# The blank rows of the last experts' slots written later, and the router's matrix of layer 2 on another queue

## The chip, the cores and the metric

The kernel runs on one core of a Trainium2 chip. A core has five engines that run beside each other, each with its own stream of instructions: TensorE (PE) for matrix products, VectorE (DVE), ScalarE (ACT), GpSimd (POOL) and SyncE (SP), which in this kernel only issues transfers. Transfers (DMAs) are issued by SP, ACT or POOL, each on its own queue, and are moved by 16 DMA engines. Engines wait for each other, and for transfers, on semaphores.

The metric is the device time of one execution in microseconds (us). Smaller is better.

## What is computed

A graph network of four layers on 3125 nodes of 256 features and 100000 edges. Each layer adds to the node rows `x` the outputs of a graph part, of a mixing part (linear attention), and then of a mixture of experts. The part that matters here is the expert part of layer 2, the graph and mixing parts of layer 3 that follow it, and the expert part of layer 3 at the end:

```python
def _L2_ffn_ref(x, Wr, br, W1, b1, W2, b2, gamma, beta):   # 8 experts, one batch
    logits = jnp.mean(x, axis=1) @ Wr + br
    routing_weights = jax.nn.softmax(logits, axis=-1)
    ...
    top_w, top_i = jax.lax.top_k(rw_tok, K)                # K = 2
    h = jax.nn.gelu(jnp.einsum('nd,edf->enf', xf, W1) + b1[:, None, :], approximate=False)
    y = jnp.einsum('enf,efd->end', h, W2) + b2[:, None, :]
    out = jnp.einsum('ne,end->nd', w_dense, y).reshape(B, S, D)
    return _layer_norm(out + x, gamma, beta)

def _L3_ffn_ref(h, gate_w, gate_b, w1, b1, w2, b2):        # 8 experts, capacity C
    ...
    buf = jnp.zeros((E, C, D), dtype=h.dtype).at[idx, pos_safe].set(x, mode='drop')
    hmid = jax.nn.relu(jnp.einsum('ecd,edf->ecf', buf, w1) + b1[:, None, :])
    ybuf = jnp.einsum('ecf,efd->ecd', hmid, w2) + b2[:, None, :]
    y_tok = ybuf[idx, pos_g] * (prb * kept)[:, None]
```

In layer 2 one routing decision holds for all nodes, since it is made from the mean over the nodes: two experts of eight are chosen, and all rows pass through both. In layer 3 every node goes to one expert, which has room for C = 489 nodes.

## The kernel before

The node rows stay on chip: `self.x` and `self.xn` (rows, 25 blocks of 125 nodes) and `self.xt` (the normalised rows turned, features on the partitions). Work on nodes goes in pieces of 500 nodes (`PIECES`), the last of 125. The source states operations in one order; a scheduler of the language then places the instructions of each engine, and it may move an instruction ahead of others of its engine where its inputs allow. What it has placed, the engine runs in that order.

`run` calls `l1_ffn`, whose last part is the graph and mixing work of layer 2, and then `l3_ffn`. `l3_ffn` does four things in this order:

1. It sets up the slots of layer 3's experts. `bx_d` in DRAM has 8 x 489 = 3912 rows of 514 numbers: the normalised row, the row itself, the weight and the node's number. Slots that no node takes must hold blank rows (zeros, and a node number out of range). One blank row is made in the tile `row` on chip (L2187, L2188, on POOL) and written to all slots of `bx_d` by two transfers on ACT's queue (L2190, L2192).
2. It defines `follow`, which routes a piece of nodes once its rows are final and scatters them into `bx_d` (L2255). It uses the same tile name `row`, of which the pool holds one buffer. So the first instruction that writes `row` again, the copy of the node numbers at L2253 (DVE), waits until the fill has read the blank row.
3. It calls `l3_gnn_mix`, which issues the loads of layer 3's weights on SP (through `l3_mix_by_pieces`, with the small columns `g1` and `b1` at L2015), then calls `l2_ffn`, and then does the graph and mixing parts of layer 3.
4. It runs the eight last experts (L2265 to L2307). For each, w1 and the slots `xb` are loaded on SP, w2 and b2 on ACT.

`l2_ffn` loads the router's matrix (L1782, on SP) and four small inputs on ACT, sums `self.mean` over the pieces (L1789), multiplies by the router's matrix (L1794), takes softmax twice and the best two (up to L975 in the helper `top2`), adds beta to `x` (`add_rows`, L982), and loads for each of the two experts W1, W2 and b1 from the place that the chosen number gives (L1819 to L1825, on SP). `expert` then runs, piece by piece, W1 (L261, PE), gelu (L1010, ACT), W2 (L1016, PE) and adds the weighted result to `y` (L1018, DVE), 25 blocks for each expert. `finish_norm` ends the layer.

Some helpers record their operations under their own lines: loads of weights L172 (`load_w`) and L179 (`load_b`), matrix products L255 and L261, copies out of PSUM L163 (DVE) and L165 (ACT), softmax L268 to L273. The sum over rows of a piece is at L1774. The loads of `cs` by layer 3's graph part are at L156.

Of the kernel before, what the change touches and what calls it, by code (L numbers as in the profile page):

```python
# [109 lines left out]
class Net:  # L110
# [1665 lines left out]
    def l2_ffn(self):  # L1776
        nc, tc, a = self.nc, self.tc, self.a
        NE = 8
        with ExitStack() as s:
            sb = s.enter_context(self.pool("f2_sb"))  # L1780
            wk = s.enter_context(self.pool("f2_wk", 2))
            wr = self.load_w(sb, "L2_ffn_Wr")  # L1782
            br = self.load_b(sb, "L2_ffn_br")
            b2 = sb.tile([NE, D], F32, name="b2")
            nc.scalar.dma_start(b2, a["L2_ffn_b2"])
            gamma = self.load_b(sb, "L2_ffn_gamma")
            beta = self.load_b(sb, "L2_ffn_beta")
            mean = sb.tile([128, HB], F32, name="mean")
            nc.vector.tensor_reduce(mean, self.mean, axis=AX.X, op=OP.add)  # L1789
            nc.vector.tensor_scalar(mean, mean, 1.0 / N, None, op0=OP.mult)  # L1790

            ps = self.bank()
            for h in range(HB):
                nc.tensor.matmul(ps[:, :NE], mean[:, h:h + 1].to_broadcast([128, 128]), wr[:, h, :],  # L1794
                                 start=(h == 0), stop=(h == HB - 1))
            rw = sb.tile([128, 1, NE], F32, name="rw")
            nc.vector.tensor_add(rw[:, 0, :], ps[:, :NE], br)
            self.softmax(sb, rw, 1, NE)
            sc = sb.tile([128, 1, NE], F32, name="sc")
            nc.vector.tensor_scalar(sc, rw, float(N), None, op0=OP.mult)  # L1800
            nc.vector.reciprocal(sc, sc)
            cap = float(-(-N * 5 // (4 * NE)))
            nc.vector.tensor_scalar(sc, sc, cap, 1.0, op0=OP.mult, op1=OP.min)
            nc.vector.tensor_mul(rw, rw, sc)
            self.softmax(sb, rw, 1, NE)
            g, tw, i8 = self.top2(sb, rw, NE, 128, 1)
            ps = self.bank()
            nc.tensor.transpose(ps[:NE, :128], g[:, 0, :], self.ident)
            gt = sb.tile([NE, 128], F32, name="gt2")
            nc.vector.tensor_copy(gt, ps[:NE, :128])  # L1810
            ps = self.bank()
            nc.tensor.matmul(ps[:P, :D], gt[:, :P], b2, start=True, stop=True)
            bb = sb.tile([P, D], F32, name="bb")
            nc.vector.tensor_copy(bb, ps[:P, :D])
            y = sb.tile([P, NB, D], F32, name="y")
            nc.vector.tensor_add(y, self.xn, self.blocks(bb))
            self.add_rows(beta)
            for j in range(2):
                e = nc.sync.value_load(i8[0:1, 0, j:j + 1], min_val=0, max_val=NE - 1)  # L1819
                w1 = wk.tile([128, HB, 512], F32, name="w1")  # L1820
                nc.sync.dma_start(w1, a["L2_ffn_W1"][ds(e, 1)].rearrange("o (c p) f -> p (o c) f", p=128))
                w2 = wk.tile([128, 4, D], F32, name="w2")
                nc.sync.dma_start(w2, a["L2_ffn_W2"][ds(e, 1)].rearrange("o (c p) f -> p (o c) f", p=128))
                b1 = wk.tile([128, 4], F32, name="b1")
                nc.sync.dma_start(b1, a["L2_ffn_b1"][ds(e, 1)].rearrange("o p f -> (o p) f"))  # L1825
                self.expert(wk, w1, b1, AF.Gelu, w2, lambda b: tw[:P, 0, j:j + 1], y)
            self.expect(1, self.norm_turn_add, 1)
            self.finish_norm(y, gamma)
# [336 lines left out]
                        nc.vector.scalar_tensor_tensor(self.x[:, b, :], t.rearrange("p h d -> p (h d)"), 0.0,  # L2165
                                                       self.x[:, b, :], op0=OP.max, op1=OP.add)

    def l3_ffn(self, before, parts):

# [5 lines left out]
        with ExitStack() as s:  # L2177
# [9 lines left out]
            nc.gpsimd.memset(blank[:, 0], 0.0)  # L2187
            nc.gpsimd.memset(blank[:, 0, WX - 1:], float(1 << 20))  # L2188
            whole = NE * CAP // 112 * 112
            nc.scalar.dma_start(bx[:whole].rearrange("(t p) d -> p t d", p=112),  # L2190
                                blank[:112, 0, None, :].to_broadcast([112, whole // 112, WX]))
            nc.scalar.dma_start(bx[whole:], blank[:NE * CAP - whole, 0])  # L2192
            place = sb.tile([P, NB], F32, name="place")
            nc.gpsimd.iota(place, pattern=[[P, NB]], base=0, channel_multiplier=1,
                           allow_small_or_imprecise_dtypes=True)
# [68 lines left out]
            tiles = [(r, min(128, CAP - r)) for r in range(0, CAP, 128)]  # L2264
            for e in range(NE):  # L2265
                w1 = self.load_w(wk, "w1", a["L3_ffn_w1"][e])
                w2 = self.load_w(wk, "w2", a["L3_ffn_w2"][e], eng=nc.scalar)
                b2 = self.load_b(wk, "b2", a["L3_ffn_b2"][e])
                xb = wk.tile([128, len(tiles), WX], F32, name="xb")
                for t, (r, n) in enumerate(tiles):  # L2270
                    nc.sync.dma_start(xb[:n, t, :], bx[e * CAP + r:e * CAP + r + n])  # L2271
                xt = wk.tile([128, HB, CAP], F32, name="xbt")
                for h in range(HB):
                    ps = self.bank()
                    for t, (r, n) in enumerate(tiles):
                        nc.tensor.transpose(ps[:, r:r + n], xb[:n, t, h * 128:(h + 1) * 128], self.ident[:n, :n])
                    self.evac(xt[:, h, :], ps[:, :CAP])
                hid = wk.tile([128, NF, CAP], F32, name="hid")
                for f in range(NF):
                    ps = self.bank()  # L2280
                    self.mm_feat(ps[:, :CAP], w1[:, :, f * 128:(f + 1) * 128], xt, 0, CAP)
                    nc.scalar.activation(hid[:, f, :], ps[:, :CAP], AF.Relu, bias=b1[:, e, f:f + 1])
                for t, (r, n) in enumerate(tiles):
                    ps = self.bank()
                    for f in range(NF):
                        nc.tensor.matmul(ps[:n, :D], hid[:, f, r:r + n], w2[:, f, :],  # L2286
                                         start=(f == 0), stop=(f == NF - 1))
                    to = wk.tile([128, 1], I32, name="to", bufs=4)
                    nc.vector.tensor_copy(to[:n], xb[:n, t, 2 * D + 1:])
                    y = wk.tile([128, D], F32, name="y")  # L2290
                    nc.vector.tensor_add(y[:n], ps[:n, :D], b2[:n])  # L2291
                    nc.vector.tensor_scalar(y[:n], y[:n], xb[:n, t, 2 * D:2 * D + 1], None, op0=OP.mult)  # L2292

                    fin = wk.tile([128, D], F32, name="fin")
                    nc.vector.tensor_scalar(fin[:n], y[:n], 0.0, 0.0, op0=OP.mult, op1=OP.is_equal)
                    num = wk.tile([128, D], F32, name="num")
                    nc.vector.tensor_tensor(num[:n], y[:n], y[:n], op=OP.is_equal)
                    sub = wk.tile([128, D], F32, name="sub", bufs=4)
                    nc.vector.tensor_scalar(sub[:n], y[:n], -1e4, 1e4, op0=OP.max, op1=OP.min)
                    nc.vector.tensor_mul(sub[:n], sub[:n], num[:n])  # L2300
                    nc.vector.copy_predicated(sub[:n], fin[:n].bitcast(U32), y[:n])  # L2301
                    nc.vector.tensor_add(sub[:n], sub[:n], xb[:n, t, D:2 * D])  # L2302
                    st = nc.gpsimd.indirect_dma_start(  # L2303
                        out=a["out"], out_offset=bass.IndirectOffsetOnAxis(ap=to[:n], axis=0),
                        in_=sub[:n], in_offset=None, bounds_check=N - 1, oob_is_err=False)
                    tc.declare_no_dep(st.ins, group="results", reason="each slot has a place of its own")
                    tc.add_to_no_dep_group("results", st.ins)  # L2307
# [32 lines left out]
    def run(self):  # L2340
        nc = self.nc
        self.prep()
        self.l0_prepare()
        self.l0_first()
        with self.pool("f0_g") as sb:
            self.l0_gates(sb)
            self.l0_gnn()
            self.l0_ffn(True)
        self.l1_ffn(self.l1_gnn_mix, self.l2_gnn_mix)
        self.l3_ffn(lambda arrivals: self.l3_gnn_mix(self.l2_ffn, arrivals), 2)  # L2350

        ps = self.bank()
        nc.tensor.matmul(ps[:, :8], self.ones, self.viol, start=True, stop=True)
        tot = self.c.tile([128, 1], F32, name="tot_v")
        nc.vector.tensor_reduce(tot, ps[:, :8], axis=AX.X, op=OP.add)
        bad = self.c.tile([128, 1], I32, name="bad_v")
        nc.vector.tensor_scalar(bad, tot, 0.0, None, op0=OP.is_gt)
        with self.tc.If(nc.values_load(bad[0:1, 0:1], min_val=0, max_val=1) != 0):
            self.general()
# [65 lines left out]
```

## Time and profile before

| what | us |
|---|---|
| median of 3 runs | 4667.59 (4659.35 to 4668.4) |
| the profiled execution | 4666.18 |
| its span, first to last instruction | 4664.4 |
| PE busy in it | 3722.3 (80%) |
| DVE busy | 2505.6 (54%) |
| ACT busy | 1302.8 (28%) |
| POOL busy | 1020.2 (22%) |

The profile comes from one execution. Its busy shares are means over stages of different kinds, so a part is read in its own stretch of time. The stages that are of interest here, in the same execution:

| stretch, us from the start | what runs |
|---|---|
| to 3251 | graph and mixing parts of layer 2 (the gathered matmuls at L1617 end here) |
| 3244 to 3279 | the blank rows are written to `bx_d` |
| 3279 to 3299 | router of layer 2 |
| 3299.5 to about 3480 | the two experts of layer 2 and the normalisation |
| 3480 to 4411 | graph and mixing parts of layer 3, routing of its pieces |
| 4411 to the end | the eight last experts |

Three kinds of lines are quoted from it. A line of windows gives, for a stretch, how long each engine was busy, the granted clock of PE as a share of full speed (PEclk), the busy share of the DMA engines, and GB/s. A line of waits names who waited, for whom, and the total, the number of times and the longest in us. A line in order of time gives start and duration in us, the engine, the line in the source, the operation with the names it writes and reads, and in brackets how long the engine stood idle before it and what ended that. A "q" behind an engine's name (ACTq, SPq) is its queue of instructions that issue transfers.

### The profile page before, as it was taken

How to read it: one execution, taken by the hardware profiler on the slowest of the kernel's cores; microseconds unless marked ns; L12 is line 12 of the kernel's file. 1: busy time of each engine (PE TensorE's matmuls, PEld its weight loads, DVE VectorE, ACT ScalarE, POOL GpSimd, SP SyncE). 2: the span in 40 equal slices, each digit the busy share in tenths (PEclk: the TensorE clock that was granted, in tenths of full speed). 3: DMA queues.
4: the chain of work that ended last, by engine and by line, in shares of the span. 5: the costliest groups of instructions: out<-in, count | busy, mean ns of one | idle time of the engine just before them, and what ended most of it. 6: DMA issues, size and time to landing. Idle time of an engine off the chain costs nothing. (4 is left out here: it accounts for less than half of the span.)

```text
span 4664.4 us, 50401 instructions
## 1 busy us (share of the span) xinstructions
PE 3722.3 (80%) x16695; PEld 2505.9 (54%) x16695; DVE 2505.6 (54%) x8604; ACT 1302.8 (28%) x2336; POOL 1020.2 (22%) x1041
## 2 busy tenths in 40 slices
PE   1887796499938799999656566766799999999698
PEld 0676695277724556555545455655464444444466
DVE  5877317544475526994322323444265666777544
ACT  1367100022213223323100000000155655555521
POOL 2000000400055000000577777775000000000011
PEclk9786896599959799999877777887899999999699
DMA  6244630244332000000333333334102222221232
GB/s 176 75 113 118 138 82 22 81 135 140 107 85 40 4 29 9 13 14 7 106 105 106 104 104 104 104 104 139 58 7 59 59 63 56 63 52 49 74 107 68
DMA packets 256035, 358.86 MB, mean 77 GB/s; under 512 B 62719, under 2 KB 199350, under 8 KB 255765
## 3 DMA queue, kind: packets, MB, share of 16 engines
q1 hardware_dynamic: 135900, 176.07, 13.1%
q0 software_dynamic: 62832, 126.93, 10.3%
q10 hardware_dynamic: 57033, 52.54, 4.2%
q8 instruction: 136, 2.23, 0.2%
q14 instruction: 134, 1.10, 0.1%
HBM read 268.73 MB, written 94.97 MB: 78 GB/s over the span
## 5 line engine op out<-in xcount | busy, mean ns | idle before, releaser
L1601 POOL DMA_INDIRECT hg<-hx_d,idx x782 | 743.3, 950 | 282.8 <-issue 214.2
L1617 PE MATMUL acc<-hg,to 128*125 128x256 f32 x2042 | 584.5, 449 | 197.9 <-DVE to L1612 192.8
L1617 PEld LDWEIGHTS acc<-hg,to 128*125 128x125 f32 x2042 | 455.4, 227 | 309.3 <-DVE to L1612 216.3
L1971 PE MATMUL acc<-z,xr 125*65 125x500 f32 (+1 forms) x1400 | 577.4, 556 | 14.3 <-DVE z L1968 13.0
L1965 ACT ACTIVATE t<-xn,us 125x1000 f32<-125x1000 f32 (+1 forms) x400 | 409.4, 1037 | 239.0 <-DVE z L1968 228.1
L1968 DVE SCALAR_TENSOR_TENSOR z<-t,us,cs 125x1000 f32<-125x1000 f32 (+1 forms) x400 | 409.3, 1028 | 115.5 <-PE acc L1971 92.6
L1971 PEld LDWEIGHTS acc<-z,xr 125*65 125x65 f32 x1400 | 188.9, 145 | 314.8 <-issue 265.5
L1605 DVE TENSOR_TENSOR kw<-hg,awt 128x8 f32<-128x8 f32 x98 | 16.4, 168 | 581.2 <-DMA hg<-hx_d,idx 513.2
L261 PE MATMUL ps<-xt,w 128*128 128x500 f32 (+1 forms) x672 | 269.0, 547 | 1.8 <-DMA w<-in_L_ffn_W_dram 1.8
L1612 DVE TENSOR_SCALAR to<-iota_w,rel_b,kw 128x125 f32<-128x125 f32 (+1 forms) x782 | 245.2, 383 | 35.6 <-PE acc L1617 28.7
L1536 DVE SCALAR_TENSOR_TENSOR junk<-iota_w,rel_b,lock 128x125 f32<-128x125 f32 (+1 forms) x782 | 248.1, 386 | 0.0
L2255 POOL DMA_INDIRECT bx_d<-row,slot x25 | 31.2, 1248 | 891.3 <-ACT t L1965 422.9
L589 PE MATMUL ps<-y,cb 125*125 125x256 bf16 x1875 | 214.7, 279 | 0.0
L589 PEld LDWEIGHTS <-cb 125*125 125x125 bf16 x1875 | 213.5, 141 | 0.1
L797 ACT ACTIVATE k<-k 125x128 f32<-125x128 f32 x50 | 15.9, 318 | 687.0 <-DVE k L796 686.9
L190 ACT ACTIVATE rstd_t<-rstd_t 125x4 f32<-125x4 f32 (+2 forms) x86 | 17.2, 203 | 645.8 <-DVE rstd_t L189 630.2
L255 PE MATMUL ps<-wo,h 128*125 128x256 f32 x800 | 187.7, 386 | 3.6 <-ACT h L1439 2.6
L243 PE MATMUL ps<-ident,xn 125*128 125x125 f32 x300 | 58.8, 347 | 159.8 <-DVE xn L209 159.7
L1445 DVE SCALAR_TENSOR_TENSOR x<-ps,lg,x 125x256 f32<-125x256 f32 x200 | 92.7, 480 | 173.6 <-PE ps L255 173.6
L261 PEld LDWEIGHTS ps<-xt,w 128*128 128x128 f32 x672 | 122.7, 193 | 114.7 <-issue 102.4
L261 PE MATMUL ps<-h,w 128*128 128x500 f32 (+1 forms) x448 | 179.5, 541 | 2.3 <-ACT h L1434 1.6
L255 PEld LDWEIGHTS ps<-wo,h 128*125 128x125 f32 x800 | 142.9, 187 | 65.9 <-ACT h L1439 43.7
(566 smaller groups left out, 6326.7 us busy)
## 6 DMA issues: line engine op xcount, KB each, us to landing
cs<-ctt_d SPq DMA_DIRECT2D x150, 218.8 KB
w<-in_L_ffn_w_dram SPq DMA_DIRECT2D x52, 512.0 KB
cnt_d<-cd SPq DMA_DIRECT2D x25, 683.6 KB
cb<-cnt_d SPq DMA_DIRECT2D x25, 683.6 KB
ctt_d<-ct ACTq DMA_DIRECT2D x6, 2734.4 KB
hg<-hx_d,idx POOLq DMA_INDIRECT x782, 2.8
b0x_d<-zero SPq DMA_DIRECT2D x1, 9984.0 KB
xb<-b0x_d SPq DMA_DIRECT2D x26, 384.0 KB
```

The costliest lines, as they stand in the source:

```text
L243: self.nc.tensor.transpose(ps[:, j * P:(j + 1) * P], src[:, i // P + j, h * 128:(h + 1) * 128], self.ident[:P, :P])
L255: self.nc.tensor.matmul(ps, xt[:, h, b * P:(b + 1) * P], w[:, h, :], start=(h == 0), stop=(h == k - 1))
L261: self.nc.tensor.matmul(ps, w[:, h, :], xt[:, h, i:i + n], start=(h == 0), stop=(h == k - 1))
L589: nc.tensor.matmul(ps[:P, :D], cf[k][:, h * P:(h + 1) * P], y3[:, b0 + k, j, :], start=(k == 0 and j == 0), stop=(k == m - 1 and j == 2))
L1445: nc.vector.scalar_tensor_tensor(self.x[:, b, :], ps[:P, :D], g[:, b, e:e + 1], self.x[:, b, :], op0=OP.mult, op1=OP.add)
L1536: nc.vector.scalar_tensor_tensor(junk[:, :m * P], self.iota_w[:, :m * P], rel[:, c:c + 1], lock[:, b:b + m].rearrange("p b n -> p (b n)"), ...
L1601: nc.gpsimd.indirect_dma_start(out=hg[:, j, :], out_offset=None, in_=hx, in_offset=bass.IndirectOffsetOnAxis(ap=idx[:, c0 + j:c0 + j + 1], ...
L1612: nc.vector.tensor_scalar(to, self.iota_w[:, :nb * P], rel[:, c:c + 1], kw[:, j:j + 1], op0=OP.is_equal, op1=OP.mult)
L1617: nc.tensor.matmul(acc[k], to[:, (k - b) * P:(k - b + 1) * P], hg[:, j, :D], start=(c == first[k]), stop=(c == last[k]))
L1965: nc.scalar.activation(t[:, :n], rows[:, k4, :n], AF.Relu, bias=us[:, 2, b, k4:k4 + 1], scale=us[:, 0, b, k4:k4 + 1])
L1968: nc.vector.scalar_tensor_tensor(z[:, :n], t[:, :n], us[:, 1, b, k4:k4 + 1], c, op0=OP.add, op1=OP.mult)
L1971: nc.tensor.matmul(acc[h, k][:, :w], xr[:, b, k4, :], z[:, k * PW:k * PW + w], start=(b == 0), stop=(b == NB - 1))
```

## The change

Four edits:

- The two transfers that write the blank rows are wrapped in a function `blank_slots`, and go on SP's queue instead of ACT's. With `later=True`, as `run` now calls it, `l3_ffn` does not issue them itself but leaves the function in `self.blank_slots`.
- `l2_ffn` calls that function after it has stated the loads for its second expert. A dependency of order alone (NoSync) on the last of these loads keeps the two transfers behind it in SP's stream; it adds no semaphore.
- The router's matrix of layer 2, `L2_ffn_Wr`, is loaded on ACT's queue instead of SP's.
- In the last experts, w2 of the second expert (`e == 1`) is loaded on SP's queue instead of ACT's.

```diff
@@ l2_ffn @@
-            wr = self.load_w(sb, "L2_ffn_Wr")
+            wr = self.load_w(sb, "L2_ffn_Wr", eng=nc.scalar)
...
-                nc.sync.dma_start(b1, a["L2_ffn_b1"][ds(e, 1)].rearrange("o p f -> (o p) f"))
+                last = nc.sync.dma_start(b1, a["L2_ffn_b1"][ds(e, 1)].rearrange("o p f -> (o p) f"))
+                if j == 1 and self.blank_slots:
+
+                    for ins in self.blank_slots():
+                        tc.add_manual_dep(ins, last.ins.name, mybir.DependencyInfo(
+                            mybir.DependencyClass.NoSync, mybir.DependencyReason.DATA), reason="weights first")
@@ l3_ffn @@
-    def l3_ffn(self, before, parts):
+    blank_slots = None
+
+    def l3_ffn(self, before, parts, later=False):
...
-            nc.scalar.dma_start(bx[:whole].rearrange("(t p) d -> p t d", p=112),
-                                blank[:112, 0, None, :].to_broadcast([112, whole // 112, WX]))
-            nc.scalar.dma_start(bx[whole:], blank[:NE * CAP - whole, 0])
+
+            def blank_slots():
+                self.blank_slots = None
+                return [nc.sync.dma_start(bx[:whole].rearrange("(t p) d -> p t d", p=112),
+                                          blank[:112, 0, None, :].to_broadcast([112, whole // 112, WX])).ins,
+                        nc.sync.dma_start(bx[whole:], blank[:NE * CAP - whole, 0]).ins]
+
+            if later:
+                self.blank_slots = blank_slots
+            else:
+                blank_slots()
...
-                w2 = self.load_w(wk, "w2", a["L3_ffn_w2"][e], eng=nc.scalar)
+                w2 = self.load_w(wk, "w2", a["L3_ffn_w2"][e], eng=nc.sync if e == 1 else nc.scalar)
@@ run @@
-        self.l3_ffn(lambda arrivals: self.l3_gnn_mix(self.l2_ffn, arrivals), 2)
+        self.l3_ffn(lambda arrivals: self.l3_gnn_mix(self.l2_ffn, arrivals), 2, True)
```

## The prediction

> **What bounds the kernel now.** I read the page first. TensorE (PE) is busy 80% of a span of 4664.4 us, so a stretch in which PE stands still is worth its length. The slices show such a stretch near 3260 us, where layer 2's expert stage begins. I then read that stretch by windows, by waits (engines, then SP's own) and in order of time.
>
> ```profile
> core 0: us, PE busy (x) PEld busy (x) DVE busy (x) ACT busy (x) POOL busy (x), PEclk, DMA share, GB/s
> 3244.00:3256.00 12.00, 7.05 (x28) 5.50 (x28) 7.94 (x21) 0.78 (x2) 0.55 (x4) 0.79 0.89 283
> 3256.00:3266.00 10.00, 0.00 (x0) 0.00 (x0) 0.00 (x0) 0.00 (x0) 0.00 (x0) 0.50 1.05 357
> 3266.00:3279.00 13.00, 0.00 (x0) 0.00 (x0) 0.00 (x0) 0.27 (x1) 0.00 (x0) 0.50 0.83 290
> 3279.00:3284.00 5.00, 0.84 (x4) 0.87 (x4) 0.85 (x4) 1.28 (x1) 0.00 (x0) 0.50 0.45 100
> 3284.00:3295.00 11.00, 0.15 (x1) 0.06 (x1) 10.13 (x31) 0.62 (x3) 0.00 (x0) 0.50 0.00 0
> ```
> For 23 us every engine is idle while the DMA engines run full; then comes a router chain with almost no DMA. The waits say on what:
> ```profile
> PE ps L1794 <- DMA L_ffn_Wr<-in_L_ffn_Wr_dram: 28.4, 1, 28.4
> ACT xt L165 <- DMA b<-in_L_ffn_b_dram: 25.1, 1, 25.1
> DVE row L2253 <- DMA bx_d<-row: 24.2, 1, 24.2
> ```
> ```profile
> SPq L2015 <- DMA bx_d<-row: 14.2, 1, 14.2
> ```
> Three engines and SP all stand behind one transfer, the blank fill of `bx_d` (7645.8 + 208.8 KB = 8.04 MB). In order of time:
> ```profile
> 3244.51 0.35 ACTq L2190 DMA_DIRECT2D bx_d<-row  x1
> ...
> 3254.80 0.29 DVE L163 COPY xt<-ps 128x125 f32<-128x125 f32 x1 [0.71 <-PE ps L243]
> ...
> 3279.24 0.17 DVE L2253 COPY row<-place 125x4 f32<-125x4 f32 x1 [24.15 <-DMA bx_d<-row]
> 3279.34 0.41 DVE L1774 TENSOR_REDUCE mean_p<-xt 128x2 f32<-128x250 f32 x1
> ...
> 3279.98 0.42 SPq L172 DMA_DIRECT2D L_ffn_Wr<-in_L_ffn_Wr_dram  x1
> ...
> 3284.67 2.35 DVE L982 TENSOR_TENSOR x<-x,L_ffn_beta 125x1024 f32<-125x1024 f32 x2
> ...
> 3295.32 0.40 SPq L1821 DMA_DIRECT2D w<-in_L_ffn_W_dram  x1
> ...
> 3299.52 9.90 PE L261 MATMUL ps<-xt,w 128*128 128x500 f32 x16 [1.84 <-DMA w<-in_L_ffn_W_dram]
> ```
> The reader should see that the input of the router (`xt`) is whole at 3255.1, its sum over rows is taken at 3279.3, and the expert's first matmul comes at 3299.5.
>
> [...] `mean` (L1774) needs nothing of `row`, yet stands 24.15 us behind it. [...] SP stood 14.2 us at L2015, and the router's matrix behind it. [...] Here the fill (ACT's queue) and layer 3's weights (SP's) moved together at 283 to 357 GB/s. [...] the trace has 0.50 in every window after 3256.
>
> **The change part by part.**
>
> *Fill off ACT's queue at 3244.5.* The wait of L2253 for it goes from in front of `mean`: in the compiled order of the changed kernel this copy stands behind the 8th accumulation `y<-ps,w,y` (L1018) of the first expert. SP's L2015 waits now for layer 3's own weights, not for the fill. These are 2.62 MB from 3248.4 on; at the 345 GB/s seen here they take 7.6 us, so SP is through by about 3260, and its next work (the expert's number) is due near 3269. Hidden, with 9 us to spare.
>
> *What is late next: the router chain.*
> - `xt` whole at 3255.1. ACT's copy of its other half no longer stands behind waits for the fill, so it comes then too.
> - L1774 to the end of L1790 took 0.82 us: 3256.0.
> - Router's matrix: now on ACT behind its copy of 3246.2 to 3246.7. It may wait for the last users of its memory, the gather stage's matmuls, which end at 3250.9. It took 3.15 us to land (3279.98 to 3283.13); in a busy stretch the 256 KB of layer 3's GNN matrix took 4.9. So it lands between 3250 and 3256: in time, within a microsecond.
> - Two matmuls to `rw` (L1797): 1.06 us, 3257.2; then L268 and L269 to the first L982: 0.48, 3257.7.
> - L982 needs beta, issued on ACT behind that copy and gamma: 3255.5. It took at most 3.47 us (3281.20 to 3284.67), so it lands at 3259.0, and the chain, which has L271 behind L982 on DVE, is held 1.3 us. I take 3259.0; with beta landing as slowly as 4.9 us it is 3260.4, with none of it 3257.7.
> - From the first L982 to the expert's weights: 3284.67 to 3295.32 = 10.65 us. The changed order still does all seven L982 ahead of L1804, so I keep it: 3269.7.
> - Weights to the first L261: 4.20 us: 3273.9. PE has been idle for 19 us, so its first 16 matmuls stay at 9.90 us rather than the 6.87 of the next piece; I count no gain there (bound: 3.0).
>
> Sum: 3299.5 - 3273.9 = 25.6 us.
>
> *Sum over rows of the last full piece (L1774, 1.19 us)* now runs ahead of L1765, in a DVE gap of 1.12 us, instead of inside the last normalisation, where it holds L191 from 3252.8 to 3253.5: 0.6 us gained, bounds 0 and 1.2.
>
> *Fill behind the second expert's weights on SP.* The three loads of the second expert begin 2.3 us after the first's and end 3.8 after them, so the fill is issued at 3273.5. The 2.10 MB of weights are ahead of it on the same queue[...]. Weights and fill together, 10.14 MB from about 3271.5 at 309 to 345 GB/s (10.7 MB moved from 3244 to 3279 is 309) end at 3301 to 3304[...]. The 8th L1018 was 30.5 us after the first L261 (3329.99), so it falls at 3304.4; the 9th, 38.9 after (3338.42), at 3312.8. DVE idles 7.95 us between them. The copy L2253 waits there for 0 to 2 us, with nothing due behind it: zero, bound 2 at the slow end[...]. Behind the fill on SP stands only `cs`, which waited 169.3 us for L1016 until 3473.84: covered. If the cover in DVE were gone, each microsecond would be one of PE[...].
>
> *w2 of layer 3's second expert from ACT to SP.* The last experts begin at 4411.05; PE's first L261 there, 4422.74, waits for `xb`, loaded by SP behind w1. On ACT, the second w2 stood behind the first w2, and SP's next w1 waited 8.6 us for a `w` until 4422.25. I take that for the first w2, still in flight; then the second had moved nothing yet and moving it gives SP no bandwidth back. If it was the second, it shared the last 1 MB of `xb`, and up to 2 us come back. On SP it now stands ahead of the second `xb`: 3.1 MB from 4422.3 at 364 to 391 GB/s land by 4431, needed at 4452. I take 0, bounds -1 (gain 2).
>
> Together 26.2 us off the profiled execution's own 4666.18 us (1.8 more than its span): 4640.0. Those runs have a median of 4667.59 (4659.35 to 4668.4), 1.4 above the profiled one; I put the forecast between the two bases, 4640.0 and 4641.4, at 4640.5.
>
> **The rivals.**
> - *Another transfer takes the fill's place (0.17).* SP's 4-byte columns at L2015, `br`, beta or the wait for freed memory in front of Wr last 6 to 16 us longer than I have them; each is on the chain one for one. For it: one load issue there took 2.78 us, and eight semaphores are shared by all loads, so one late load holds others. Against it: those delays fall beside the fill. 10 to 20 us left: 4648 to 4658, middle 4653.
> - *More than counted (0.10).* Beta in time, PE warm sooner, the `xb` head 2 us earlier: 1.3 + 3.0 + 2, saving 32: 4634.
> - *The fill holds the experts: slower (0.05).* L2253 sits between two L1018. If fill and weights need more than 41 us (from 3271.5 to 3312.8), every further microsecond stalls DVE, the banks and PE. All the gain is gone from 3339 on, that is with the 10.14 MB at 150 GB/s. At 125 GB/s it lands at 3353 and costs 40: 4666.2 - 26.2 + 40 = 4680. Against it: the three windows in which the fill ran show 283 to 357.
> - *It doesn't do what it says (0.03).* The copy in DVE or the wait in SP keeps the old order, and time stays at 4667. The compiled order speaks against it.
> - *As summed (0.65).* 20 to 30 us off: 4636 to 4647.
>
> **How the numbers follow.** About 0.2%, 9.3 us, can be told from no change. Faster: 0.65 + 0.10 + 0.16 of the first rival = 0.91. Within: 0.03 + its last 0.01 = 0.04. Slower: 0.05. The range takes in the main case, the greater gain down to 4631 and the middle of the first rival: 4631 to 4654; likeliest alone 4636 to 4647.
>
> **What would show it.** Right: DVE's wait for `bx_d<-row` is gone before 3260, L1794 starts near 3256, the first L261 of that stage near 3274, and the stage after it is as long as before. The fill runs from about 3277 to 3304 beside L1016, with L2253 behind the 8th L1018 and no DVE wait of more than 8 us before the 9th. Wrong: a wait over 5 us for a load in front of L1794, L982 or SP's L1821; a gap in PE between L1018's 8th and 9th; a later start of the last experts than 26 us ahead of before.

## The result, and the profile after

| | before | after |
|---|---|---|
| median of 5 runs, us | 4667.27 (4659.35 to 4668.4) | 4645.13 (4636.11 to 4653.43) |
| the profiled execution, us | 4666.18 | 4653.43 |
| its span, us | 4664.4 | 4651.7 |

The ratio of after to before is 0.9956, with a 95% interval of 0.994 to 0.9972: 0.28% to 0.6% less, or 13 to 28 us of 4667. Five more runs of the changed kernel, taken later beside the experiments, had a median of 4644.19 against 4668.66 for the kernel before, ratio 0.9949 (0.9937 to 0.9962).

The two profiled spans differ by only 12.7 us, less than the medians do. The changed kernel's profiled execution was already 10.4 us late when it reached the part that was changed, in code that both kernels share. So times from the start can't be laid side by side. I count instead from one event ahead of the change: the start of ACT's last square root over a whole piece (L190, 125x4), at 3243.50 before and 3253.92 after. "The stretch" below is the time from this event to the first L261 of layer 2's experts. The numbers of this table are differences of start times in the two traces (in the last row, to the end of the span), in us:

| part | before | after |
|---|---|---|
| event to `mean` (L1790) | 36.49 | 12.13 |
| event to the router's matmuls (L1794) | 39.66 | 16.32 |
| event to the first expert's weights issued (L1821) | 51.82 | 28.40 |
| event to the first L261: the stretch | 56.02 | 32.46 |
| first L261 to layer 3's first `cs` load | 174.32 | 174.17 |
| `cs` to the last scatter into `bx_d` | 934.15 | 934.29 |
| last scatter to the last experts' first L261 | 14.75 | 15.62 |
| from there to the end of the span | 241.7 | 241.2 |

The stretch became 23.56 us shorter; the four parts behind it together became 0.4 us longer. The gain is where it was looked for, and 2.6 us short of the 26.2 that were forecast.

The windows of the changed kernel (columns as before: the stretch, its length, busy us of PE, PE's weight loads, DVE, ACT and POOL, the clock, the share of the DMA engines and GB/s):

```profile
3254.00:3266.00 12.00, 6.89 (x28) 5.49 (x28) 8.79 (x25) 1.18 (x5) 0.78 (x4) 0.80 0.47 144
3266.00:3271.00 5.00, 0.76 (x4) 0.79 (x4) 0.19 (x2) 1.27 (x1) 0.00 (x0) 0.50 0.79 238
3271.00:3282.00 11.00, 0.23 (x2) 0.14 (x1) 10.08 (x32) 0.62 (x3) 0.00 (x0) 0.50 0.10 25
...
3290.00:3300.00 10.00, 10.00 (x32) 6.11 (x31) 2.74 (x3) 3.60 (x5) 0.00 (x0) 0.90 1.06 377
3300.00:3310.00 10.00, 10.00 (x33) 5.90 (x32) 1.08 (x3) 2.24 (x4) 0.00 (x0) 1.00 1.04 352
```

The 23 us in which every engine was idle are gone. What is left of them is the second line: 5 us with almost nothing on any engine while DMA runs at 238 GB/s. The fill is in the last two lines: 377 and 352 GB/s, and PE busy in all of both. The order in time shows who waited in that second line.

```profile
3258.85 0.39 SPq L172 DMA_DIRECT2D L_mix_Wq<-in_L_mix_Wq_dram  x1
...
3260.82 2.06 SPq L172 DMA_DIRECT2D L_mix_W<-in_L_mix_W_dram  x2
...
3262.40 0.40 DVE L1201 TENSOR_REDUCE wx<-wx_t 128x4 f32<-128x256 f32 x1
...
3262.88 0.39 ACTq L172 DMA_DIRECT2D L_ffn_Wr<-in_L_ffn_Wr_dram  x1
3265.51 0.44 ACTq L179 DMA_DIRECT2D L_ffn_beta<-in_L_ffn_beta_dram  x1
3266.05 0.17 DVE L1790 TENSOR_SCALAR mean<-mean 128x2 f32<-128x2 f32 x1
...
3270.24 0.99 PE L1794 MATMUL ps<-L_ffn_Wr,mean 128*128 128x8 f32 x4 [5.54 <-DMA L_ffn_br<-in_L_ffn_br_dram]
...
3271.75 1.22 DVE L982 TENSOR_TENSOR x<-x,L_ffn_beta 125x1024 f32<-125x1024 f32 x1
...
3282.32 0.40 SPq L1821 DMA_DIRECT2D w<-in_L_ffn_W_dram  x1
...
3317.10 0.16 DVE L2268 COPY row<-place 125x4 f32<-125x4 f32 x1
3325.13 0.48 DVE L1018 SCALAR_TENSOR_TENSOR y<-ps,w,y 125x256 f32<-125x256 f32 x1 [7.87 <-PE ps L1016]
```

The `mean` is there at 3266.22, the matmul with the router's matrix starts at 3270.24: 4.0 us late for the matrix. The wait names `br`, which was issued right behind it on ACT and which this matmul does not read; in the second profiled execution of this kernel (experiment 5) the same wait names the matrix. By the trace's semaphore events the matrix had landed at 3270.05. ACT issued it 0.08 us after the end of DVE's last L1201. L1201 belongs to the preparation of layer 3: it sums over `wx_t`, a tile of the pool `m3_w`, which the source closes just before `l2_ffn` opens its own pools. PE had the matrix 7.4 us after its issue, beside layer 3's weights that SP had started 4.0 to 2.1 us earlier. The last two lines are the copy that used to wait for the fill, and the accumulation after it. The copy runs without a wait, and DVE then still idles 7.87 us before its next accumulation.

### The profile page after: what moved, and what is told of

It is laid out like the page before. It is cut to its first block, busy times and chain, and to the rows that moved or that the text cites. A ratio compares the mean times of both kernels' runs of the same rounds, so it can differ in the third digit from the quotient of the medians.

```text
span 4651.7 us, 50402 instructions
## 1 busy us (share of the span) xinstructions
PE 3730.8 (80%) x16695; PEld 2512.0 (54%) x16695; DVE 2507.1 (54%) x8604; ACT 1302.0 (28%) x2336; POOL 1020.1 (22%) x1041
## 3 DMA queue, kind: packets, MB, share of 16 engines
q0 software_dynamic: 62832, 126.93, 10.4%
## 5 line engine op out<-in xcount | busy, mean ns | idle before, releaser
L1976 PE MATMUL acc<-z,xr 125*65 125x500 f32 (+1 forms) x1400 | 577.4, 555 | 14.4 <-DVE z L1973 13.1
L261 PE MATMUL ps<-xt,w 128*128 128x500 f32 (+1 forms) x672 | 268.9, 547 | 1.8 <-DMA w<-in_L_ffn_W_dram 1.8
L190 ACT ACTIVATE rstd_t<-rstd_t 125x4 f32<-125x4 f32 (+2 forms) x86 | 17.2, 203 | 648.7 <-DVE rstd_t L189 631.7
L261 PEld LDWEIGHTS ps<-xt,w 128*128 128x128 f32 x672 | 122.7, 193 | 114.6 <-issue 102.2
L261 PE MATMUL ps<-h,w 128*128 128x500 f32 (+1 forms) x448 | 179.5, 541 | 2.3 <-ACT h L1434 1.6
```

What stands on the lines that cost most here:

```text
L261: self.nc.tensor.matmul(ps, w[:, h, :], xt[:, h, i:i + n], start=(h == 0), stop=(h == k - 1))
L1976: nc.tensor.matmul(acc[h, k][:, :w], xr[:, b, k4, :], z[:, k * PW:k * PW + w], start=(b == 0), stop=(b == NB - 1))
```

## The experiments

All stretches are counted from the same event, each in its own profile. A single time says little (the five runs of the changed kernel cover 17 us), so the stretches carry the readings.

**1. Only DVE freed.** The kernel before, with the blank row in a tile of its own, so that L2253 waits for nothing:

```diff
-            blank = wk.tile([P, 4, WX], F32, name="row")
+            blank = wk.tile([P, 1, WX], F32, name="blank")
```

> Kernel before with one edit: the blank row has a tile of its own, so that the copy of node numbers into row no longer waits for the fill. The stretch read is that from ACT's last rstd of a full piece (125x4) to the first expert matmul of layer 2: 56.0 us before, 32.5 after the change. Theory A (the fill holds three queues at once: DVE's copy, ACT's copy of xt behind its small loads, SP's router matrix behind L2015): nothing is won by freeing DVE alone, stretch 54 to 57. Theory B (DVE's copy in front of the mean is what held the router): stretch 32 to 38.

The stretch was 56.6 us, as in theory A, and the time 4668.65 us against 4663.53 of the kernel before on the same chip: nothing gained. Waits in the stretch:

```profile
PE ps L1794 <- DMA L_ffn_Wr<-in_L_ffn_Wr_dram: 27.7, 1, 27.7
ACT xt L165 <- DMA L_ffn_br<-in_L_ffn_br_dram: 24.4, 1, 24.4
DVE mean_p L1774 <- ACT xt L165: 22.5, 1, 22.5
```

DVE no longer waits for `bx_d`, but for ACT's half of `xt`, for 22.5 us instead of 24.2. That copy stands on ACT behind the issue of the fill's second, small part, which got out only 22.5 us after the first (3252.80 and 3275.29 in that trace), and behind the three loads that follow it there (what these wait for is read in experiment 2). The fill held the stage by two ways at once, through the tile on DVE and through ACT's queue (and SP's L2015 besides); taking one away wins nothing.

**2. The fill left early, the router's inputs ahead of it.** Own tile as in 1, and the router's matrix, `br`, `b2` and `beta` loaded on ACT before the fill, in memory that is free then:

```diff
+    def l2_small(self, sb):
...
+            wr, br, b2, beta = self.small or self.l2_small(sb)
...
+            gamma = self.load_b(sb, "L2_ffn_gamma", eng=nc.sync)
...
+                self.small = self.l2_small(sb)
...
+            blank = wk.tile([P, 1, WX], F32, name="blank")
```

> Kernel before, the fill still early on ACT, but the blank row in a tile of its own and the router's matrix, br, b2 and beta of layer 2 loaded at the start of l3_ffn, long before; gamma on SP. So the router waits for none of its inputs, and the DMA engines are as full as before. Theory A (waits in the queues): the router comes earlier, up to what still stands behind the fill, SP's L2015 until about 35 us after the stretch's start and ACT's copy of xt behind the second part of the fill; stretch 40 to 45. Theory C (the full DMA engines themselves set the time): stretch 52 or more. If DVE and the small loads were all of it: 31 to 34.

The stretch was 43.5 us, as in theory A, and the time 4655.41 (before 4663.53). A good half of the gain comes without moving the fill, but not from the freed waits alone: with beta there early, the scheduler placed the additions (L982) ahead of the router, so that from `mean` to L975 it took 6.4 us instead of 15.4 (3.0 of which had been the wait for the matrix). ACT in order of time shows what still holds `mean`:

```profile
3251.20 0.34 ACTq L2197 DMA_DIRECT2D bx_d<-blank  x1
...
3274.32 0.48 ACTq L2199 DMA_DIRECT2D bx_d<-blank  x1
3274.84 0.27 ACT L165 COPY xt<-ps 128x125 f32<-128x125 f32 x1 [14.03 <-DMA L_mix_Wm<-in_L_mix_Wm_dram]
```

Line numbers are shifted by 7. The small second part gets out 23 us behind the first, and the last piece's `xt` copy follows it at once. What ACT waited for is named in the bracket, and it is not the fill: it is `L_mix_Wm`, a load of layer 3's weights on SP. The semaphore events of the trace say the same. The second part waited for a semaphore that this load uses too, the load landed at 3274.30, and the issue came at 3274.32. In the kernel before the two times are 3266.23 and 3266.25, in experiment 1 3275.27 and 3275.29, and there `br` and `b2` behind it waited in the same way for the two loads of `L_mix_W`. Beside the fill `L_mix_Wm` took 12.4 to 13.1 us from issue to landing in these three kernels, and 4.0 to 5.7 in the eight profiles with the fill late. So the fill slows the loads that move beside it, and these hold ACT's stream through semaphores that they share with its own transfers. This is read from the traces; no run takes the shared semaphore out alone.

SP holds the end of the stretch:

```profile
SPq L2020 <- DMA bx_d<-blank: 13.5, 1, 13.5
```
```profile
3282.21 0.17 DVE L975 TENSOR_TENSOR g<-g,h 128x8 f32<-128x8 f32 x1
...
3288.88 0.40 SPq L1825 DMA_DIRECT2D w<-in_L_ffn_W_dram  x1
```

The router has chosen at 3282.38, but the first expert's weights are issued 6.5 us later, since SP's remaining small loads had waited for the fill until 3285.26. (In the changed kernel L1821 is issued as L975 starts.) So two queues hold what is left, and not the router's inputs, which were there.

**3. Only the fill moved.** The changed kernel with the router's matrix still on SP and w2 still on ACT (the diff of `blank_slots` alone). The "second last expert" of the expectations is the second of the eight last experts, `e == 1`.

> Changed kernel with the two other edits undone: the router's matrix on SP again, w2 of the second last expert on ACT again. Theory A: the fill's move is nearly all of it; the router's matrix then stands behind layer 3's loads on SP and lands about 20 us after the stretch's start against 16.3, so stretch 34 to 38 (32.5 with the matrix on ACT, 56.0 before). Rival: the matrix's queue is what counts, stretch 50 or more. From the last scatter into bx_d to the first matmul of the last experts: 14.8 us, as before, if the moved w2 costs (15.6 after the change); no change from 15.6 if it doesn't.

The stretch was 33.6 us, just under theory A's 34 to 38, and the time 4645.48 us. So the fill's place is nearly the whole gain (22.4 us of the stretch). With the matrix on ACT the stretch is 0.4 to 1.1 us shorter (33.2 and 32.5 in two profiles of the changed kernel), hardly more than the 0.7 by which those two differ. The matrix itself came 3.7 us later here: L1794 starts 20.0 us after the event, against 16.3. Most of that does not show, because the scheduler put four of the seven additions of beta ahead of the router's first step on DVE (3266.79 to 3271.42), so fewer of them stand behind it. From the last scatter to the last experts' first L261 it took 16.15 us with w2 on ACT, which neither of the two forecasts for it had; experiment 6 takes it for spread.

**4. Is the fill really covered?** The changed kernel with the fill's large part written twice:

```diff
-                return [nc.sync.dma_start(bx[:whole].rearrange("(t p) d -> p t d", p=112),
+                first = nc.sync.dma_start(bx[:whole].rearrange("(t p) d -> p t d", p=112),
+                                          blank[:112, 0, None, :].to_broadcast([112, whole // 112, WX])).ins
+                return [first, nc.sync.dma_start(bx[:whole].rearrange("(t p) d -> p t d", p=112),
```

> Changed kernel, the large part of the fill written twice (7.8 MB more behind the second expert's weights; the scheduler then sets DVE's copy behind the 16th accumulation of the first expert instead of the 8th). Theory A: the fill is hidden with room; stretch 32.5 as after the change, and the two experts, from the first L261 to the first cs load, as long as before (174 us), though DMA runs full for some 52 us of them. Rival: full DMA engines slow the experts, or the copy holds DVE, 10 us or more longer.

The stretch was 33.3 us and the experts took 173.7 (174.2 with one fill), as in theory A; 4652.52 us in all. Windows of that run, through the experts:

```profile
3295.00:3305.00 10.00, 10.00 (x39) 6.95 (x38) 1.88 (x4) 2.03 (x3) 0.00 (x0) 1.00 1.05 372
3305.00:3320.00 15.00, 15.00 (x55) 10.08 (x54) 2.13 (x5) 2.71 (x4) 0.00 (x0) 1.00 0.81 276
3320.00:3346.00 26.00, 26.00 (x93) 17.18 (x92) 3.68 (x8) 5.42 (x8) 0.00 (x0) 1.00 0.90 296
```

7.8 MB more, and PE is never idle. One thing limits the reading: in this kernel the scheduler put the copy of the node numbers behind the 16th L1018 (3347.43), and the second fill ended near 3345. It shows that the transfer as such costs PE nothing, not that DVE could wait that long behind the 8th. In the changed kernel the fill had landed at 3315.53 (the trace's semaphore events), 1.6 us before the copy at 3317.10.

**5. What held the router's chain.** Four kernels, two edits in all combinations (the one with both also has w2 back on ACT, which lies behind the stretch). "Early" loads the matrix and `br` at the start of `l3_ffn`, into memory that is free then; "behind" puts the seven additions of beta (L982) behind `y` (L1816) on DVE by a dependency of order alone:

```diff
-            wr = self.load_w(sb, "L2_ffn_Wr", eng=nc.scalar)
-            br = self.load_b(sb, "L2_ffn_br")
+            wr, br = self.router or (self.load_w(sb, "L2_ffn_Wr", eng=nc.scalar), self.load_b(sb, "L2_ffn_br"))
...
+                self.router = self.load_w(sb, "L2_ffn_Wr", eng=nc.scalar), self.load_b(sb, "L2_ffn_br")
```
```diff
-            nc.vector.tensor_add(y, self.xn, self.blocks(bb))
-            self.add_rows(beta)
+            made = nc.vector.tensor_add(y, self.xn, self.blocks(bb))
+            self.add_rows(beta, made)
```

The changed kernel itself, once more:

> The changed kernel once more, beside the variants below on the same chip. Theory A (the router's matrix waits for freed memory, whatever the run): from the last full piece's L190 to the first L261 of layer 2's experts 31.5 to 33.5 us as before (32.5), the matrix issued within 0.3 us after DVE's last L1201 and over 3 us late for L1794. Theory B (that lateness was a chance of one execution): 29 to 30 us, with the matrix there within 1 us of the mean. Total 15 to 28 us under the kernel before in either.

The matrix early:

> The changed kernel with the router's matrix and br loaded at the start of the last expert part, into memory that is free at that time, nothing else changed. Theory A (waiting for freed memory is what made the matrix late, and nothing stands close behind it): L1794 follows the mean within 0.5 us, the stretch to the first L261 is 28.5 us (32.5 less the 4.0 that L1794 waited). Theory B (beta, issued behind the same wait, takes the place): L982 waits for beta, stretch 30 to 32. Theory C (the matrix's load is not what held the chain): 32.5 as it was.

The additions behind `y` (run last and on another chip, with the results of the other three known):

> The changed kernel with only the seven additions of beta (L982) placed behind y (L1816); the router's matrix stays behind its wait for freed memory. Stretches so far: 32.5 to 33.2 us (changed kernel), 32.7 (matrix early alone), 23.5 (matrix early and additions behind y). Theory A (two late loads side by side: matrix and beta each hold the chain, and one was hidden behind the other): the additions take 5 to 6 us out of the chain, the matrix's 4 us stay, stretch 26.5 to 28. Theory B (the additions' place is worth all of it, the matrix nothing): 23 to 24.5. Theory C (beta still holds the chain in another way): over 30. Experts 173 to 174.5 as in the others.

Both, and w2 back on ACT:

> The changed kernel with the router's matrix and br loaded early as in the run before, the seven additions of beta (L982) placed behind y (L1816) instead of inside the router chain, and w2 of the second last expert back on ACT. Theory A (the router chain is a pure chain, and DVE has room in the first expert's pieces for the 7.7 us of L982): stretch to the first L261 22 to 24 us (32.5 less 4.0 for the matrix, less 5 to 6 for L982), experts 173.5 to 175 us as before, total 8 to 10 us under the changed kernel. Theory B (the additions now hold the first accumulations L1018 and with them the banks of PE): same stretch, but experts 177 to 182, total 1 to 5 us under or no gain. Theory C (something else holds the chain, the expert's weights or SP): stretch above 27.

| stretch, us | additions in the chain | additions behind `y` |
|---|---|---|
| matrix behind the wait for memory | 32.5, 33.2 | 26.4 |
| matrix early | 32.7 | 23.5 |

The changed kernel again was late by the same place (theory A): L1794 4.3 us behind the mean, and the matrix issued less than 0.1 us after the last L1201, as in all five profiles with the matrix behind that wait. With the early load L1794 followed the mean within 0.1 us (3267.00 to 3267.10). And yet the early matrix alone gained nothing in the stretch (4647.7 us in one run), for this is what came next (DVE and ACT of that kernel in order of time):

```profile
3264.50 1.33 ACTq L179 DMA_DIRECT2D L_ffn_beta<-in_L_ffn_beta_dram  x1
...
3266.83 0.17 DVE L1790 TENSOR_SCALAR mean<-mean 128x2 f32<-128x2 f32 x1
3267.10 0.99 PE L1794 MATMUL ps<-L_ffn_Wr,mean 128*128 128x8 f32 x4 [2.05 <-DMA L_mix_W<-in_L_mix_W_dram]
...
3271.20 2.36 DVE L982 TENSOR_TENSOR x<-x,L_ffn_beta 125x1024 f32<-125x1024 f32 x2 [2.51 <-DMA L_ffn_beta<-in_L_ffn_beta_dram]
```

DVE stands 2.51 us in front of L982 for beta, which sits behind the same wait for memory on ACT, and the router's L271 is queued behind L982: its input from ACT (L270) was ready at 3268.93, and it ran at 3273.48, behind the first two L982. The first L982 starts 17.85 us after the event here, 17.83 in the changed kernel. There beta had landed at 3271.42 (the trace's semaphore events), 0.33 us before L982: matrix and beta are equally late, so each was hidden behind the other. The stretch alone fits theory C's 32.5; the trace shows the wait of theory B, longer than its 30 to 32 us allowed for. With the additions out of the chain (26.4 us, 0.1 under theory A's 26.5 to 28; 4642.02 in one run, beside 4661.62 of the kernel before) the matrix is worth 2.9 us (26.4 to 23.5).

The wait that goes is about 4, but in the two early kernels `mean` itself came at 13.3 to 13.5 us instead of 11.8 to 12.4, as in experiments 3 and 4. The traces say why: in these four PE's granted clock from 2.7 to 9 us after the event, while the last gathered matmuls run, was 0.64 to 0.74, and these matmuls ended 8.5 to 9.0 us after the event; in the other four profiles with the fill late it was 0.87 to 0.91, and they ended at 7.4 to 7.6. Why the clock differs there stays open. Counted from the end of `mean` instead, the way to the first L261 is 20.2 and 20.6 us in the changed kernel, 19.1 with the matrix early, 14.1 with the additions behind `y`, and 10.0 with both. So the early matrix is worth 1.1 to 1.5 us with the additions in the chain, and 4.1 without them.

Both edits together, as in theory A (23.5 us): DVE goes through the router without a stop for a load and does the additions beside the first expert's matmuls.

```profile
3268.48 0.17 DVE L1793 TENSOR_SCALAR mean<-mean 128x2 f32<-128x2 f32 x1
...
3274.61 0.17 DVE L975 TENSOR_TENSOR g<-g,h 128x8 f32<-128x8 f32 x1
...
3284.05 7.23 DVE L982 TENSOR_TENSOR x<-x,L_ffn_beta 125x1024 f32<-125x1024 f32 x7
3291.20 0.87 DVE L1021 SCALAR_TENSOR_TENSOR y<-ps,w,y 125x256 f32<-125x256 f32 x2
```

(L1021 is L1018 of the kernel before.) From mean to L975 it takes 6.1 us; in the changed kernel, 16.3 (3266.05 to 3282.36). The first two accumulations run back to back behind the additions, so they had been waiting, but the experts took 173.4 us: nothing is lost. This version had a median of 4636.41 us in six runs (4626.57 to 4640.55), ratio to the kernel before 0.9924 (0.9913 to 0.9936), beside 4644.19 and 0.9949 (0.9937 to 0.9962) of the changed kernel on the same chip. The intervals don't touch: it is 7.8 us faster than the changed kernel by medians, just under the 8 to 10 expected, and 9.0 to 9.7 by the stretch, and it beats both.

**6. w2 back on ACT.** The changed kernel without its last edit:

```diff
-                w2 = self.load_w(wk, "w2", a["L3_ffn_w2"][e], eng=nc.sync if e == 1 else nc.scalar)
+                w2 = self.load_w(wk, "w2", a["L3_ffn_w2"][e], eng=nc.scalar)
```

> The changed kernel with only w2 of the second last expert back on ACT. Theory A (the move neither gains nor costs): from the last scatter to the first L261 of the last experts 14.7 to 16.2 us, the spread of the runs so far, whichever side w2 is on. Theory B (the move on SP costs): 13.5 to 14.7. Theory C (the move gains): over 16.5. The rest as in the changed kernel.

From the last scatter to the first L261 it took 15.44 us, as in theory A. With w2 on SP the five profiles have 15.62, 15.36, 16.05, 15.34 and 15.56, with it on ACT and the fill late 16.15, 15.44 and 15.26: means of 15.59 and 15.62. The edit neither gains nor costs. (The three kernels with the fill early, w2 on ACT, have 14.75, 15.11 and 14.95, so this part is some 0.7 us longer with the fill late, whichever side w2 is on; why stays open.) The single time, 4637.26, is the lowest of the variants with this stretch (32.5 us), but the profile shows it earlier already at the event (3243.81), in code that is the same; it is spread, and no effect of w2.

## Why the prediction was right, and which term was off

The forecast was 4640.5 us; the two medians are 4645.13 and 4644.19. Its range held both. Still, two of its own signs of being wrong appeared: PE waited 5.54 us for a load in front of L1794 (over 5), and the last experts started 22.7 us earlier, counted from the event, instead of 26. By its own steps:

- *What held the stage before.* In part misread. `xt` was not whole at 3255.1: that is DVE's half, and ACT's half was copied at 3277.82. So of the 24.15 us that `mean` stood behind the copy into `row`, it could have used only the last 1.2. The clearer case of an instruction that is ready and stands behind one that waits is L271 behind L982 in experiment 5. ACT's part of the hold came through layer 3's loads (experiment 2). The step that followed, that the fill must go from both, does not depend on it.
- *The fill off ACT's queue.* Right. DVE's wait for `bx_d` and ACT's long wait in front of its copy are gone. Experiment 1 shows that freeing DVE alone is not enough.
- *SP hidden, with 9 us to spare.* Right: SP waited 9.7 us for the expert's number, after issuing its last column at 3270.69.
- *The router's matrix lands in time, within a microsecond.* Wrong, and the step that failed. It was priced at 3.15 us to land, 4.9 in a busy stretch, from a wait for memory that ends with the gather's matmuls at 3250.9, 7.4 us after the event. These did end there (7.5), but the load waited for DVE's last L1201 as well, on layer 3's `wx_t`, until 8.9 us after the event, and then took 7.4 us. PE waited 4.0 us for it.
- *Beta holds the chain 1.3 us.* Not seen in the changed kernel, where L982 follows L269 at once. Beta was late too, and more than forecast: it landed 17.5 us after the event, where the forecast had 15.5. But the matrix was as late and hid it (in the kernel with the matrix early L982 waits 2.51 us for it). Both inputs stand behind the same wait on ACT's queue.
- *From the first L982 to the weights 10.65, then 4.20.* Measured 10.57 and 4.06.
- *The sum over rows of the last full piece, 0.6 us gained.* The end of `mean` came 12.30 us after the event; the forecast, with its 0.6, was 11.9. About 0.2 of it came by this count, which says little, since `mean` comes 11.8 to 13.5 us after the event in the eight profiles with the fill late.
- *PE's first 16 matmuls stay at 9.90.* 9.76, at a mean granted clock of 0.71 (9.90 at 0.70 in the kernel before, whose next 16 took 6.87 at 1.00).
- *Fill hidden behind the experts, cost 0.* Right: the copy L2268 ran behind the 8th L1018 with no wait, and the 9th came 38.75 us after the first L261 (38.9 before). The forecast's end of the transfer, 3301 to 3304, is 57.5 to 60.5 us after the event; here the last packet of the fill moved at 3315.15, 61.2 us after it, and its landing was signalled at 3315.53. The weights ahead of it on SP's queue had all landed 10.3 us after the first of them was issued, 9.1 before; the first took 4.0 (4.2 before). The 0 to 2 us for the copy were the author's estimate, as was that a longer hold in DVE would cost PE each microsecond: the latter no run showed.
- *w2 moved, cost 0.* Right, by experiment 6. In the kernel before the first w2 landed at 4422.23, and the second, 1 MB issued behind it on ACT, 3.4 us later (4425.67).
- *The sums.* They come out but for roundings: 3255.1 and 0.82 are 3255.9, with 1.06 and 0.48 behind them the first L982 is at 3257.5 and not 3257.7. Beta's 3259.0 stands behind it in either case, so the 25.6 does not change. The 309 GB/s are 307.

Between forecast and trace the stretch thus differs by 2.6 us: 0.4 more for `mean`, 3.8 more for the matrix (the 4.0 less the 0.2 from the matrix's landing, 3270.05, to PE's start), 1.3 less for beta, 0.2 less in the two last steps: 2.7, and 0.1 of rounding. The other 1 to 2 us between the forecast and the medians are within what five runs scatter. So the total came as near as it did partly by luck: the matrix's 3.8 us were softened by beta's 1.3, which the forecast had counted and which the matrix hid.

Of the rivals, the one in which another transfer takes the fill's place is there in kind, but at 2.6 us net instead of 10 to 20: its places were in part named rightly (memory in front of the matrix, beta). It had each of them on the chain one for one. The runs show that these two delays on one queue don't add up: the matrix and beta covered each other. PE's first 16 matmuls got no faster, and the experts no slower, so neither the rival with more gain nor the one with the fill holding the experts came true.

## What to carry to other kernels

When a large transfer holds a stage, list all the ways in which it does (a shared tile, loads that it slows and that other transfers wait for, another engine's queue): with only one of them gone (experiment 1) the stretch took 56.6 us here, and 56.0 before. Read what a wait names before you blame the queue it stands in. A small input that is loaded just in time into memory that was used before comes only after the last reader of that memory, plus a landing in traffic (here issued 0.08 us after the last L1201, and used 7.4 us later); if it can be had early, load it early, and with all the others that sit behind the same wait, or the next of them takes its place (beta, for 2.51 us). On the chain to a decision keep only what the decision needs: here 7.7 us of additions that nobody was waiting for cost 6 us or more when they stood inside it and nothing behind it.

## What the runs showed of the hardware

- An issue right behind a large transfer on the same queue held its engine for 18 of the 29 us that this transfer took. On SP of the changed kernel the first part of the fill was issued in 0.38 us, the second, of 209 KB, in 17.91:

```profile
3286.23 0.38 SPq L2200 DMA_DIRECT2D bx_d<-row  x1
3286.66 17.91 SPq L2202 DMA_DIRECT2D bx_d<-row  x1
```

  It was 17.7 to 19.6 in the other runs with one fill behind the weights. The semaphore that it waits for had long been ready (3273.84), so the time is in the issue. It ended at 3304.57, the fill at 3315.5. SP has nothing else to do there. On ACT, in the kernel before and in experiments 1 and 2, the second part is another case: its issue took 2.16, 1.05 and 0.48 us, and came late because of the semaphore of `L_mix_Wm`.
- A load's landing can hold transfers that have nothing to do with it. With one set of eight semaphores for the transfers of SP and ACT, the second part of the fill was issued 0.02 us after `L_mix_Wm` had landed, in three kernels (experiment 2).
- The fill ran at 352 to 377 GB/s beside PE at 90 to 100% of its clock and did not lengthen the experts: 174.2 us with it, 174.3 without, 173.7 with two.
- From issue to the matmul that reads it, the matrix, 8 KB, took 3.15 us in the kernel before, with 100 GB/s of other traffic (3279 to 3284), and 7.4 us in the changed kernel beside 2.6 MB on SP's queue (6.5 to 7.8 in five profiles with it on ACT). It is not the queue alone: beta, 128 KB and on ACT in both kernels, landed 3.0 and 5.9 us after its issue.
